# Edge tiles over 64 nodes with fixed node ranges in a four-layer graph network kernel

## The chip, the core and the metric

The kernel runs on one core of a Trainium2 chip, as one program and one launch. The metric is device microseconds per execution. TensorE multiplies matrices, VectorE and ScalarE do elementwise work and reductions, GpSimd does some elementwise work and issues the indirect gathers, and SyncE issues most of the other transfers.

## The reference

Four layers over a graph of N = 2048 nodes, for B = 8 batches of D = 64 features. The adjacency `adj` is an integer matrix, symmetric, with ones on its diagonal; it is random and sparse (each of the two halves that are joined has a chance of 0.00195 per entry, so a node has about nine neighbours). After each layer the input is added and a layer norm follows.

```python
# layer 0, attention with one score per side
h = layernorm((x * node_weights + node_bias + x) @ W) * gamma + beta
e = leaky_relu(s1[:, :, None] + s2[:, None, :], 0.2)     # s1 = h @ a1, s2 = h @ a2
out = elu(softmax(where(adj > 0, e, -9e15)) @ h + h)
# layer 1, softmax over the neighbours, for each feature by itself
feat = softplus(x * (w0 / sqrt(2)) + b0);  scores = feat * wa + ba
out = sum over j of softmax_j(where(adj, scores[j], -1e9)) * feat[j]
# layer 2, mean over the neighbours
out = layernorm(relu(x @ W_self + b_self + (adj @ x / deg) @ W_neigh + b_neigh))
# layer 3, four heads and a last layer, both with scores h_i . h_j over the neighbours
h = x @ Wh[head].T;  out_h = softmax(where(adj, h @ h.T, -1e16)) @ h      # for 4 heads
h2 = leaky_relu(concat(out_h), 0.2) @ Wo.T
out2 = softmax(where(adj, h2 @ h2.T, -1e16)) @ h2 + bo
out = layernorm(leaky_relu(out2, 0.2)) * gamma + beta
# after each layer: x = layernorm(x + out)
```

## The kernel before

The nodes form 16 node tiles of 128 (`P`). All neighbours of a node tile are put into **edge tiles** of 128 slots, one slot for one edge. A node tile is cut into `NG` groups of `GN` = 32 nodes, and each group has `GS` = 3 edge tiles, 384 slots (`GE`). A group's two halves of `GH` = 16 nodes each start at a fixed slot, 0 and 192: so the first edge tile holds edges of the first half only, the second of either half, and the third of the second half only. `src` (L173) holds for each slot the row of the source node, `SelT` the matrix from nodes to slots, and `Sel` its transpose. `gather` (L186) is an indirect transfer that GpSimd issues: it fetches for the 128 slots of an edge tile the rows of their source nodes from a table in device memory. A node tile takes 12 gathers.

The program's stages, in order:

- **Adjacency and node products (L303 to L383).** For each node tile VectorE finds the neighbours in the adjacency rows (`key`, `MAX8`), TensorE counts the slots ahead of each node (`pl`, L354), VectorE makes `offs` and `ends`, `first_of` (L362) and `SelT` (L363), TensorE spreads the lists to the slots (`pl`, `ps`, L369 and L370), ScalarE copies `Sel` (L371), and VectorE reads each slot's neighbour out (`hit`, `at_`, `src`). A matrix form of the adjacency, `ET`, is kept for the first `DENSE` node tiles. The products of layer 0 run in between.
- **Layer 0 (L385 to L470).** For each node tile: 12 gathers into `hs` (two buffers), scores, weights, `weigh` (L421: VectorE multiplies the gathered rows by the weights, L428, and TensorE sums them with `self_`, a copy of `Sel`, into `po`, and the weights into `pd`), `divide`, residual and norm. While the gathers of a node tile go out, the one before is worked on.
- **Layer 1 and layer 2 sums (L556 to L620, L880 to L945).** The first `DENSE` = 9 node tiles are summed by dense matmuls with `ET` (L556, L915; 24 and 12 of 512 columns in a batch). The other node tiles are summed by list: gathers of `rs`, then matmuls with `self_` (L608, L895) in "quads" of four edge tiles, one of each group, that write four different column groups of 32. TensorE's order alternates dense batches with quads.
- **Heads of layer 3 (L954 to L1190).** For each edge tile: `fetch` the rows `xs`, `turn` them (four transposes into `pt`, L1000, and a copy `xsT` on ScalarE, L1002), `score` (matmuls `pscore`, L1015, an exp on ScalarE, L1018, and a mask by `Sel` on VectorE, L1024), and `back` (matmuls of the weights with the rows into `po`, L1041, and a copy into `o` on VectorE, L1046). Edge tiles 0 and 2 of a group, each over 16 nodes, form one step, and edge tile 1, over 32 nodes, the next; there are eight steps per node tile. Beside them runs the work of whole node tiles: `turn_nodes` (transposes of X), `sides` (`quarters` L970 and copies into `U`), `through_w` (`quarters` of `o`, and z), `sums` (a transpose of the softmax sums, L1058, and reciprocals), `through_wo` (L1076, and h2 on VectorE and GpSimd) and `pieces` (three bfloat16 parts of h2). The order on TensorE, ScalarE, VectorE and GpSimd is the order of the program, written out by hand: `turn(k+2)`, work aside, `score(k+1)`, `back(k)`. `beside` says which work stands in which step j of a node tile. The PSUM banks: `pt` one, `pscore` two buffers of two banks, `po` one, `pm` (for `quarters`, Wo and `turn_nodes`) two.
- **Last layer (L1186 to L1345).** Units of two gathers, six per node tile: TensorE expands the nodes' own rows to the slots (`pe`, L1210), VectorE multiplies (`pr`, L1215) and reduces (`sc`, L1220), ScalarE takes the exp, the weighting `wx` is shared by VectorE and ScalarE in two units of three and done by GpSimd in the third (L1231, L1236), and TensorE adds up (`po`, `pd`, L1248, L1250). The end work of a node tile (`divide`, `leaky`, `take_stats`, `normalise`, ...) stands at fixed units after it. Here too the order is the program's.

At the end a few operations see whether any node had too many neighbours, or any slot range ran over; in that case a slower program for any input runs (`nbad`, L1354 and after).

Of the kernel before, what the change touches and what calls it, by code (L numbers as in the profile page):

```python
# [32 lines left out]
P = 128  # L33
# [15 lines left out]
def kernel(ctx: ExitStack, tc: tile.TileContext, ins: dict, out: bass.AP):  # L49
# [12 lines left out]
    GN = 32  # L62
    GH = 16
    NG = P // GN
    GS = 3
    GE = GS * P
    SL = 24

# [99 lines left out]
    room = main.tile([P, 1], F32, name="room")  # L168
# [3 lines left out]
    Sel = main.tile([P, NT, GS, P], FP8, name="Sel")  # L172
    src = main.tile([P, NT, GS, NG], U32, name="src")  # L173
    recs = main.tile([P, NT, HN + 1, B], F32, name="recs")
# [7 lines left out]
    DENSE = 9  # L182
# [122 lines left out]
    nc.vector.tensor_scalar(before, before, 0.0, None, op0=ALU.is_gt)  # L305
    half_i = aw.tile([P, 1], I32, name="half_i")
    nc.gpsimd.iota(half_i, pattern=[[0, 1]], base=0, channel_multiplier=1)
    nc.vector.tensor_scalar(half_i, half_i, 4, None, op0=ALU.logical_shift_right)
    half_no = aw.tile([P, 1], F32, name="half_no")
    nc.vector.tensor_copy(half_no, half_i)  # L310
    halves = aw.tile([P, P // GH, GH], F32, name="halves")
    nc.gpsimd.iota(halves, pattern=[[1, P // GH], [0, GH]], base=0, channel_multiplier=0, allow_small_or_imprecise_dtypes=True)
    nc.vector.scalar_tensor_tensor(before, halves.rearrange("p a b -> p (a b)"), half_no, before,
                                   op0=ALU.is_equal, op1=ALU.mult)
    nc.vector.tensor_scalar(half_i, half_i, 1, None, op0=ALU.bitwise_and)
    half0 = aw.tile([P, 1], F32, name="half0")
    nc.vector.tensor_copy(half0, half_i)
    nc.vector.tensor_scalar(half0, half0, GE / 2, None, op0=ALU.mult)
    nc.vector.tensor_scalar(room, half0, GE / 2, None, op0=ALU.add)
# [3 lines left out]
    for it in range(NT):  # L323
# [28 lines left out]
        pl = aps.tile([P, 1 + GS * NG * (SL + 1)], F32, name="pl", bufs=1)  # L352
        poff = pl[:, 0:1]
        nc.tensor.matmul(poff, before, deg[:, it:it + 1], start=True, stop=True)  # L354
        nc.vector.tensor_scalar(offs[:, it:it + 1], poff, half0, 2.0 * GE, op0=ALU.add, op1=ALU.min)
# [9 lines left out]
        pl = pl[:, 1:].rearrange("p (g l) -> p g l", l=SL + 1)  # L365
        ps = aps.tile([P, GS, P], F32, name="ps", bufs=1)
# [4 lines left out]
        nc.scalar.activation(Sel[:, it], ps, AF.Copy, saturate=False)  # L371
# [7 lines left out]
        nc.vector.tensor_reduce(at_.rearrange("p s g -> p (s g)"), hit, AX.X, ALU.add)  # L379
        nc.vector.tensor_scalar(src[:, it], at_, -1.0, 0.0, op0=ALU.add, op1=ALU.max)  # L380
# [13 lines left out]
    def fetch(it):  # L394
# [6 lines left out]
        self_ = wk.tile([P, GS, P], F32, name="self_")  # L401
# [19 lines left out]
    def weigh(it):  # L421
        hs, self_, w, wm = held[it]
        po = ps_o.tile([P, BD], F32, name="po")
        pd = ps_w.tile([P, NG, B], F32, name="pd")
        for s in range(GS):
            own = slice(s * NG, (s + 1) * NG)
            wx = hs[:, own].rearrange("p g b d -> p (g b) d")
            nc.vector.tensor_tensor(wx, wx, along(w[:, own].rearrange("p g b -> p (g b)")), ALU.mult)  # L428
            nc.tensor.matmul(pd, self_[:, s], wm[:, own], start=(s == 0), stop=(s == GS - 1))
            for g in range(NG):  # L430
                nodes = slice(g * GN, (g + 1) * GN)
                nc.tensor.matmul(po[nodes], self_[:, s, nodes], hs[:, s * NG + g].rearrange("p b d -> p (b d)"),
                                 start=(s == 0), stop=(s == GS - 1))
        held[it] = po, pd

    def divide(it):
        po, pd = held.pop(it)
        den = wk.tile([P, NG, B], F32, name="den")
        nc.vector.tensor_tensor(den, pd, group.unsqueeze(2).to_broadcast(den.shape), ALU.mult)
        rd = wk.tile([P, B], F32, name="rd")  # L440
        nc.vector.tensor_reduce(rd, den.rearrange("p g b -> p b g"), AX.X, ALU.add)
        nc.vector.reciprocal(rd, rd)
        z = zs[it] = po.rearrange("p (b d) -> p b d", d=D)
        for b in range(B):
            nc.scalar.activation(z[:, b], z[:, b], AF.Copy, scale=rd[:, b:b + 1])
# [55 lines left out]
    with ExitStack() as l1:  # L501
# [87 lines left out]
        quads = [(it, s) for it in range(NT - 1, DENSE - 1, -1) for s in range(GS)]  # L589
        rss, selfs = {}, {}  # L590

        def fetch(n):
            if n < len(quads):
                it, s = quads[n]
                rss[n] = [gk.tile([P, 2, BD], F32, name="rs") for _ in range(NG)]
                for g in range(NG):
                    gather(rss[n][g].rearrange("p h n -> p (h n)"), rtab, it, s, g)

        def add_edges(n):
            it, s = quads[n]  # L600
            if s == 0:
                selfs[it] = wk.tile([P, GS, P], F32, name="self_")
                nc.scalar.activation(selfs[it], Sel[:, it], AF.Copy)
                sums[it] = new_sums()
            for h in range(2):
                for g in range(NG):
                    nodes = slice(g * GN, (g + 1) * GN)
                    nc.tensor.matmul(sums[it][h][nodes].rearrange("p a f -> p (a f)"), selfs[it][:, s, nodes],  # L608
                                     rss[n][g][:, h], start=(s == 0), stop=(s == GS - 1))
            if s == GS - 1:  # L610
# [26 lines left out]
    f3w = fast.enter_context(tc.tile_pool(name="f3w", bufs=1))  # L637
    early = ExitStack()
# [13 lines left out]

    def turn_nodes(it):
# [4 lines left out]
        nc.scalar.copy(xTs[it], px.rearrange("p a n -> p (a n)"))  # L658
        for k in range(2):
            nc.vector.memset(xTs[it][k * D:k * D + 1], 1.0)  # L660
# [51 lines left out]
    with ExitStack() as l2:  # L712
# [160 lines left out]
        quads = [(it, s) for it in by_list for s in range(GS)]  # L873

        def selection(n):
            if n < len(by_list):
                it = by_list[n]
                selfs[it] = wk.tile([P, GS, P], F32, name="self_", bufs=3)
                nc.scalar.activation(selfs[it], Sel[:, it], AF.Copy)

        def fetch(n):
            if n < len(quads):
                it, s = quads[n]
                rss[n] = [gk.tile([P, BD], F32, name="rs") for _ in range(NG)]
                for g in range(NG):
                    gather(rss[n][g], ytab, it, s, g)

        def add_edges(n):
            it, s = quads[n]
            if s == 0:  # L890
                selection(by_list.index(it) + 2)
                sums[it] = pa.tile([P, BD], F32, name="pa")
            for g in range(NG):
                nodes = slice(g * GN, (g + 1) * GN)
                nc.tensor.matmul(sums[it][nodes], selfs[it][:, s, nodes], rss[n][g], start=(s == 0), stop=(s == GS - 1))  # L895
            if s == GS - 1:
# [55 lines left out]
    with early, ExitStack() as heads:  # L952
        wk = heads.enter_context(tc.tile_pool(name="f3s", bufs=2))
        gk = heads.enter_context(tc.tile_pool(name="f3g", bufs=13))  # L954
        ps_t = heads.enter_context(tc.tile_pool(name="f3pst", bufs=1, space=PSUM))
        ps_s = heads.enter_context(tc.tile_pool(name="f3pss", bufs=2, space=PSUM))
        ps_o = heads.enter_context(tc.tile_pool(name="f3pso", bufs=1, space=PSUM))
# [3 lines left out]
        def quarters(W, v, hs, pool=None):  # L961


            pq = pool.tile([P, 2, 2, 2, P], F32, name="pscore") if pool else ps_m.tile([P, 2, 2, 2, P], F32, name="pm")
# [17 lines left out]


        NODES = [(0, GH), (0, GN), (GH, GH)]
        PARTS = ((0, 2), (1,))
        steps = [(it, g, ss) for it in range(NT) for g in range(NG) for ss in PARTS]

        def fetch(k):
            it, g, ss = steps[k]
            xss[k] = [gk.tile([P, BD], F32, name="xs") for _ in ss]  # L990
# [927 lines left out]
```

## Time and profile before

| | |
|---|---|
| median of 3 runs | 2062.78 us (2061.77 to 2065.36) |
| span of the profiled execution | 2152.0 us |
| TensorE busy | 1601.9 us, 74% |
| VectorE busy | 1410.2 us, 66% |
| GpSimd busy | 1065.8 us, 50% |
| ScalarE busy | 1024.4 us, 48% |
| moved by DMA | 283.66 MB, 132 GB/s in the mean |

The profile is one execution taken by the hardware profiler; its span is 4.3% above the median of the runs. The page gives no other time for the profiled execution than this span, so every sum over profile rows is to be compared with 2152.0. Its busy shares are averages over stages with different limits, so the stages have to be read one by one: in the profile, the adjacency stage runs from 0 to 205 us, layer 0 to 511, layer 1's rows to 615, layer 1's sums to 786, layer 2's node products to 841, layer 2's sums to 1037, the heads to 1728, the last layer to the end. Rows of groups give line, engine, operation, out<-in, shapes and count, then busy time and mean nanoseconds of one, then the idle time ahead and what ended it. Float32 matmuls show as two records each, and durations of TensorE records overlap, so the text takes the distance of their starts.

### The profile page before, as it was taken

How to read it: one execution, taken by the hardware profiler on the slowest of the kernel's cores; microseconds unless marked ns; L12 is line 12 of the kernel's file. 1: busy time of each engine (PE TensorE's matmuls, PEld its weight loads, DVE VectorE, ACT ScalarE, POOL GpSimd, SP SyncE). 2: the span in 40 equal slices, each digit the busy share in tenths (PEclk: the TensorE clock that was granted, in tenths of full speed). 3: DMA queues.
4: the chain of work that ended last, by engine and by line, in shares of the span. 5: the costliest groups of instructions: out<-in, count | busy, mean ns of one | idle time of the engine just before them, and what ended most of it. 6: DMA issues, size and time to landing. Idle time of an engine off the chain costs nothing. (4 is left out here: it accounts for less than half of the span.)

```text
span 2152.0 us, 35076 instructions
## 1 busy us (share of the span) xinstructions
PE 1601.9 (74%) x13062; PEld 921.8 (43%) x13062; DVE 1410.2 (66%) x3027; ACT 1024.4 (48%) x2506; POOL 1065.8 (50%) x997
## 2 busy tenths in 40 slices
PE   3562334442799988876599999899999859888873
PEld 3552111110333345222487777777777712222220
DVE  6887477876664466467255555555555569898986
ACT  4542134346822243364354444444444436677774
POOL 0001766661655536554445455545544367777760
PEclk9755666555999999998599999999999955555555
DMA  7422666550258833554333223323322155555541
GB/s 197 142 85 73 198 181 183 176 176 23 96 181 292 303 114 110 161 150 118 90 90 113 78 89 99 103 83 98 99 84 84 60 168 166 162 168 170 164 120 27
DMA packets 134243, 283.66 MB, mean 132 GB/s; under 512 B 64144, under 2 KB 66704, under 8 KB 131984
## 3 DMA queue, kind: packets, MB, share of 16 engines
q0 software_dynamic: 64896, 217.10, 33.4%
q1 hardware_dynamic: 52528, 60.03, 8.3%
q10 hardware_dynamic: 16640, 4.20, 0.9%
q8 instruction: 105, 1.72, 0.3%
q14 instruction: 74, 0.61, 0.1%
HBM read 245.35 MB, written 35.91 MB: 131 GB/s over the span
## 5 line engine op out<-in xcount | busy, mean ns | idle before, releaser
L186 POOL DMA_INDIRECT hs<-htab,src x192 | 183.8, 957 | 290.6 <-PE pe L408 202.8
L1024 DVE SCALAR_TENSOR_TENSOR w<-w,Sel 128x512 f32<-128x512 f32 (+1 forms) x192 | 188.6, 1009 | 193.8 <-ACT w L1018 192.8
L186 POOL DMA_INDIRECT xs<-xtab,src x192 | 216.4, 1127 | 76.3 <-issue 39.0
L556 PE MATMUL pa<-R,ET 128*128 128x512 bf16 x864 | 198.9, 388 | 51.9 <-POOL R L544 35.0
L1015 PE MATMUL pscore<-U,xsT 64*128 64x64 f32 (+1 forms) x3072 | 224.2, 288 | 10.4 <-issue 7.9
L186 POOL DMA_INDIRECT hs<-ktab,src x192 | 188.7, 983 | 53.8 <-issue 46.6
L1015 PEld LDWEIGHTS pscore<-U,xsT 64*128 64x128 f32 x3072 | 198.4, 196 | 36.4 <-issue 25.7
L1018 ACT ACTIVATE w<-pscore 128x1024 f32<-128x1024 f32 x128 | 131.0, 1023 | 144.7 <-PE pscore L1015 112.1
L1002 ACT COPY xsT<-pt 128x512 f32<-128x512 f32 x192 | 112.1, 584 | 178.5 <-PE pt L1000 134.6
L1041 PE MATMUL po<-w,xs 128*64 128x64 f32 (+1 forms) x3072 | 159.6, 251 | 17.6 <-DVE o L1046 13.4
L151 ACT ACTIVATE X<-X,ln_m,ln_r 128x64 f32<-128x64 f32 x256 | 87.2, 428 | 171.3 <-DVE ln_m L143 66.9
L1086 POOL TENSOR_TENSOR h<-h,h2h 128x512 f32<-128x512 f32 x45 | 57.1, 1269 | 221.3 <-DVE h2h L1082 221.0
L1210 PE MATMUL pe<-hi,selTb 32*128 32x512 bf16 x576 | 135.9, 606 | 35.0 <-DVE pr L1215 26.2
L556 PEld LDWEIGHTS <-ET 128*128 128x128 fp8e4 x864 | 84.1, 99 | 174.3 <-issue 82.5
L1041 PEld LDWEIGHTS po<-w,xs 128*64 128x64 f32 x3072 | 127.5, 142 | 52.4 <-issue 28.9
L1000 PE MATMUL pt<-ident,xs 128*128 128x128 f32 x768 | 134.3, 301 | 20.5 <-DMA xs<-xtab,src 12.3
L1215 DVE TENSOR_TENSOR pr<-pe,hs 128x1024 f32<-128x1024 f32 x96 | 116.9, 1218 | 18.2 <-DMA hs<-ktab,src 9.9
L1231 ACT ACTIVATE wx<-hs,w 128x64 f32<-128x64 f32 x512 | 128.7, 341 | 0.0
L1220 DVE TENSOR_REDUCE sc<-pr 128x16 f32<-128x1024 f32 x96 | 116.6, 1215 | 4.3 <-ACT w L1222 1.2
L186 POOL DMA_INDIRECT rs<-rtab,src x84 | 79.7, 949 | 72.2 <-PE pa L608 52.1
L1000 PEld LDWEIGHTS pt<-ident,xs 128*128 128x128 f32 x768 | 86.1, 148 | 49.0 <-issue 13.3
L428 DVE TENSOR_TENSOR hs<-hs,w 128x2048 f32<-128x2048 f32 x48 | 106.8, 2279 | 0.5 <-ACT w L418 0.5
(597 smaller groups left out, 3243.1 us busy)
## 6 DMA issues: line engine op xcount, KB each, us to landing
at<-in_adj SPq DMA_DIRECT2D x16, 1024.0 KB
rtab<-r SPq DMA_DIRECT2D x16, 512.0 KB
ptab<-hp SPq DMA_DIRECT2D x16, 384.0 KB
hi<-ptab SPq DMA_DIRECT2D x16, 384.0 KB
X<-in_x ACTq DMA_DIRECT2D x16, 256.0 KB
htab<-H SPq DMA_DIRECT2D x16, 256.0 KB
ytab<-y SPq DMA_DIRECT2D x16, 256.0 KB
ktab<-hb SPq DMA_DIRECT2D x16, 256.0 KB
```

Source lines behind the costliest of these rows:

```text
L186: nc.gpsimd.indirect_dma_start(out=dst, out_offset=None, in_=table[:, :], in_offset=bass.IndirectOffsetOnAxis(ap=src[:, it, s, g:g + 1], a ...
L556: nc.tensor.matmul(po[h].rearrange("p a f -> p (a f)"), ET[:, jt, it * P:(it + 1) * P], R[:, jt, q, h].rearrange("p a f -> p (a f)"), star ...
L1000: nc.tensor.transpose(pt[:, p], xss[k][n][:, p * P:(p + 1) * P], ident)
L1002: nc.scalar.copy(xsT, pt)
L1015: nc.tensor.matmul(pscore[:, k_, f0:f0 + HN * ni].rearrange("p (h i) -> p h i", i=ni), xsTs[k][t][half, p], Us[it][half, p, :, i0:i0 + ni] ...
L1018: nc.scalar.activation(w.rearrange("p t k a h i -> p k t (a h i)"), pscore.rearrange("p k (t m) -> p k t m", t=n), AF.Exp)
L1024: nc.vector.scalar_tensor_tensor(wt, wt, 3.0e38, edge, op0=ALU.min, op1=ALU.mult)
L1041: nc.tensor.matmul(po[half, p, :, i0:i0 + ni], xss[k][t][:, f0:f0 + D], ws[k][:, t, k_, p], start=(s == 0 and p == 0), stop=(last and p == ...
L1210: nc.tensor.matmul(pe[:, k].rearrange("p b d -> p (b d)"), selTb[nodes, s * P:(s + 1) * P], hi[nodes, q], start=(q == 0), stop=(q == 2))
L1215: nc.vector.tensor_tensor(pr.rearrange("p k b d -> p (k b d)"), pes[u].rearrange("p k b d -> p (k b d)"), hss[u].rearrange("p k b d -> p ( ...
L1220: nc.vector.tensor_reduce(sc, pr, AX.X, ALU.add)
L1231: nc.scalar.activation(wxs[u][:, 0, b], hss[u][:, 0, b], AF.Copy, scale=ws[u][:, 0, b:b + 1])
```

## The change

Groups get 64 nodes (`GN`), so there are two per node tile, with five edge tiles each (`GS`, 640 slots): ten gathers per node tile instead of twelve. Each edge tile may hold edges of a fixed range of nodes only (`WINDOWS`: 0 to 20, 10 to 32, 20 to 44, 32 to 54, 44 to 64 of the 64). The lower 32 nodes (a "block") fill the slots from the front, the upper 32 from the end. A selection matrix is kept per pair of edge tile and block, `QS`, six per group: edge tile 2 belongs to both blocks. All sums write 32 output rows at a time; `TOGETHER` puts edge tiles 0 and 3, 1 and 4, and 2 together, so that a round again writes four column groups.

In layer 0, `pd` is summed per block, so that `den` and its reduction are left out. Layers 1 and 2 take 8 node tiles by matrix (`DENSE`) and 8 by list. In the heads a step is one edge tile, in the order 0, 2, 1, 4, 3, ten steps per node tile; `back` stands one step later (after `score(k+1)` comes `back(k-1)`); the sums of a block have a `po` bank each of two; `quarters` moves from `pm` to the buffers of `pscore`, `sums` from `ps_t` to `pm`, which now has one bank; one piece of work aside stands in each step; the ones in `xT` come from ScalarE's copy (scale and bias) instead of two memsets on VectorE; z is copied by ScalarE, and VectorE takes the maximum of z and 0.2 z. In the last layer a unit is the two gathers of one edge tile number, five units per node tile. The checks at the end also count each group's edges and the offsets from the end.

```diff
-    GN = 32
-    GH = 16
+    GN = 64
+    GB = 32
     NG = P // GN
-    GS = 3
+    GS = 5
...
+    WINDOWS = [(0, 20), (10, 32), (20, 44), (32, 54), (44, 64)]
+    def blocks_of(s):
+        a, b = WINDOWS[s]
+        return [(k, max(a, k * GB), min(b, (k + 1) * GB)) for k in range(GN // GB) if a < (k + 1) * GB and b > k * GB]
...
+    TOGETHER = ((0, 3), (1, 4), (2,))
+    QS = [(s, x[0]) for s in range(GS) for x in blocks_of(s)]
...
-    Sel = main.tile([P, NT, GS, P], FP8, name="Sel")
+    Sel = main.tile([P, NT, NG, NQ, GB], FP8, name="Sel")
...
-    DENSE = 9
+    DENSE = 8
...
-        nc.vector.tensor_scalar(offs[:, it:it + 1], poff, half0, 2.0 * GE, op0=ALU.add, op1=ALU.min)
+        nc.vector.tensor_scalar(offs[:, it:it + 1], poff, -1.5 * GE, 2.0 * GE, op0=ALU.max, op1=ALU.min)
+        nc.vector.tensor_tensor(offs[:, it:it + 1], offs[:, it:it + 1], base, ALU.add)
...
-        nc.scalar.activation(Sel[:, it], ps, AF.Copy, saturate=False)
+        for k in range(GN // GB):
+            of = [q for q, x in enumerate(QS) if x[1] == k]
+            nc.scalar.activation(Sel[:, it, :, of[0]:of[-1] + 1].rearrange("p g q n -> p q g n"),
...
+        nc.vector.tensor_scalar(at_, at_, float(N), None, op0=ALU.min)
...
     def weigh(it):
...
-        pd = ps_w.tile([P, NG, B], F32, name="pd")
-        for s in range(GS):
-            own = slice(s * NG, (s + 1) * NG)
...
+        pd = ps_w.tile([P, B], F32, name="pd")
+        for n, ss in enumerate(TOGETHER):
+            for s in ss:
+                own = slice(s * NG, (s + 1) * NG)
+                wx = hs[:, own].rearrange("p g b d -> p (g b) d")
+                nc.vector.tensor_tensor(wx, wx, along(w[:, own].rearrange("p g b -> p (g b)")), ALU.mult)
...
     def divide(it):
-        den = wk.tile([P, NG, B], F32, name="den")
-        nc.vector.tensor_tensor(den, pd, group.unsqueeze(2).to_broadcast(den.shape), ALU.mult)
-        nc.vector.tensor_reduce(rd, den.rearrange("p g b -> p b g"), AX.X, ALU.add)
-        nc.vector.reciprocal(rd, rd)
+        nc.vector.reciprocal(rd, pd)
...
-        nc.scalar.copy(xTs[it], px.rearrange("p a n -> p (a n)"))
-        for k in range(2):
-            nc.vector.memset(xTs[it][k * D:k * D + 1], 1.0)
+        nc.scalar.activation(xTs[it], px.rearrange("p a n -> p (a n)"), AF.Identity, scale=keep[:, 0:1], bias=keep[:, 1:2])
...
-        quads = [(it, s) for it in by_list for s in range(GS)]
+        quads = [(it, c) for it in by_list for c in range(len(TOGETHER))]
...
-        gk = heads.enter_context(tc.tile_pool(name="f3g", bufs=13))
+        gk = heads.enter_context(tc.tile_pool(name="f3g", bufs=12))
-        ps_o = heads.enter_context(tc.tile_pool(name="f3pso", bufs=1, space=PSUM))
+        ps_o = heads.enter_context(tc.tile_pool(name="f3pso", bufs=2, space=PSUM))
...
-            pq = pool.tile([P, 2, 2, 2, P], F32, name="pscore") if pool else ps_m.tile([P, 2, 2, 2, P], F32, name="pm")
+            pq = ps_s.tile([P, 2, 2, 2, P], F32, name="pscore")
...
-        NODES = [(0, GH), (0, GN), (GH, GH)]
-        PARTS = ((0, 2), (1,))
-        steps = [(it, g, ss) for it in range(NT) for g in range(NG) for ss in PARTS]
+        TURN = (0, 2, 1, 4, 3)
+        steps = [(it, g, s) for it in range(NT) for g in range(NG) for s in TURN]
+        OPEN, CLOSE = (0, 2), (1, 3)
...
-            pd = ps_t.tile([P, 2 * HN * NP], F32, name="pt")
+            pd = pool.tile([P, 2 * HN * NP], F32, name="pt") if pool else misc([P, 2 * HN * NP])
...
-            nc.scalar.activation(z.rearrange(flat), pn.rearrange(flat), AF.Relu, scale=0.8)
-            nc.vector.scalar_tensor_tensor(z.rearrange(flat), pn.rearrange(flat), 0.2, z.rearrange(flat), op0=ALU.mult, op1=ALU.add)
+            nc.scalar.copy(z.rearrange(flat), pn.rearrange(flat))
+            nc.vector.scalar_tensor_tensor(z.rearrange(flat), z.rearrange(flat), 0.2, z.rearrange(flat), op0=ALU.mult, op1=ALU.max)
...
-            0: lambda it: ([(turn_nodes, it + 1)], []),
-            1: lambda it: ([(through_w, it - 1, 0)], []),
-            2: lambda it: ([(sums, it - 1)], [(through_wo, it - 1, 0)]),
-            3: lambda it: ([(through_wo, it - 1, 1)], [(through_w, it - 1, 2)]),
-            4: lambda it: ([], [(through_wo, it - 1, 2)]),
-            5: lambda it: ([(through_wo, it - 1, 3)], [(sides, it + 1, 0)]),
-            6: lambda it: ([], [(sides, it + 1, 2)]),
-            7: lambda it: ([(pieces, it - 1)], []),
+            0: (turn_nodes, 1), 1: (through_w, -1, 0), 2: (sides, 1, 0), 3: (through_w, -1, 2), 4: (through_wo, -1, 0),
+            5: (through_wo, -1, 1), 6: (sides, 1, 2), 7: (through_wo, -1, 2), 8: (through_wo, -1, 3), 9: (pieces, -1),
...
-        AHEAD = 6
+        AHEAD = 7
...
-            for k in range(len(steps)):
+            for k in range(len(steps) + 1):
...
-                    turn(k + 2, 0)
-                it = steps[k][0]
-                aside(k % (NG * len(PARTS)), it, 0)
+                    turn(k + 2)
+                it, j = divmod(k, PER)
+                if j == 4 and 0 < it < NT:
+                    sums(it - 1)
+                f, t, *a = beside[j]
+                if k < len(steps) and 0 <= it + t < NT:
+                    f(it + t, *a)
                 if k + 1 < len(steps):
                     score(k + 1)
-                if k + 2 < len(steps):
-                    turn(k + 2, 1)
-                aside(k % (NG * len(PARTS)), it, 1)
-                back(k)
+                if k:
+                    back(k - 1)
...
-        units = [(it, s, g) for it in range(NT) for s in range(GS) for g in range(0, NG, 2)]
+        units = [(it, s) for it in range(NT) for s in range(GS)]
...
-        PER = GS * NG // 2
+        PER = GS
...
-        lack = fp.tile([P, 3, NT], F32, name="lack")
+        lack = fp.tile([P, 5, NT], F32, name="lack")
```

## The prediction

> **What bounds the kernel now.** I read the chain that ended last first: no engine has over 9% of it and no line over 4%, so there is no single bound and the work goes stage by stage. The table of busy time by stretch comes next. Its columns are the stretch, its length, the busy time of TensorE, weight loads, VectorE, ScalarE and GpSimd, then the granted clock, the DMA share and GB/s.
>
> ```profile
> 0.00:205.00 205.00, 95.00 (x594) 83.98 (x594) 170.36 (x696) 92.81 (x157) 3.24 (x12) 0.72 0.40 124
> 205.00:511.00 306.00, 126.55 (x576) 49.57 (x576) 215.68 (x389) 103.82 (x322) 183.80 (x192) 0.59 0.56 165
> 615.00:786.00 171.00, 166.74 (x917) 63.75 (x914) 94.64 (x239) 41.10 (x119) 79.51 (x95) 1.00 0.76 259
> 841.00:1037.00 196.00, 146.19 (x660) 52.28 (x658) 114.95 (x417) 88.73 (x242) 97.01 (x105) 0.88 0.46 133
> 1037.00:1728.00 691.00, 630.32 (x8506) 520.29 (x8507) 359.48 (x486) 312.52 (x433) 335.12 (x283) 0.93 0.30 91
> 1728.00:2152.00 424.00, 325.00 (x1334) 88.71 (x1333) 353.42 (x665) 276.44 (x1070) 278.54 (x247) 0.52 0.50 144
> ```
>
> These are A (adjacency and node products; VectorE), B (layer 0), D (layer 1 sums; TensorE 97%), F (layer 2 sums; TensorE and gathers), G (heads of layer 3; TensorE 91%) and H (its last layer; VectorE 83%). The two stretches between them have no edge tiles. In A, VectorE idles only 14 us at the start and otherwise for short waits.
>
> In B no engine is full. GpSimd's waits there:
>
> ```profile
> POOL hs L186 <- issue: 51.5, 169, 0.3
> POOL hs L186 <- remote: 33.9, 14, 3.1
> ```
>
> Gathers leave back to back, 0.96 us busy and 0.30 of issue each, and stop once per node tile for 2.4 us before its first one. `hs` has two buffers, so that stop is the older node tile's sums giving its buffer back. A node tile takes 17.3 us.
>
> In G, a timeline of TensorE shows what an edge tile costs (start, busy time, group; I use start to start):
>
> ```profile
> 1446.69 1.09 PE L1041 MATMUL po<-w,xs 128*64 128x128 f32 x16
> 1447.72 0.66 PE L1000 MATMUL pt<-ident,xs 128*128 128x128 f32 x4
> 1448.31 1.16 PE L1015 MATMUL pscore<-U,xsT 64*128 64x128 f32 x16
> ...
> 1451.06 1.15 PE L1041 MATMUL po<-w,xs 128*64 128x64 f32 x32
> 1452.14 0.66 PE L1000 MATMUL pt<-ident,xs 128*128 128x128 f32 x4
> 1452.63 1.06 PE L1076 MATMUL pm<-WoT,z 128*128 128x128 f32 x8
> 1453.62 2.00 PE L1015 MATMUL pscore<-U,xsT 64*128 64x64 f32 x32
> ```
>
> A 32-node tile (x16) scores in 1.14 us and sums in 1.03. Two 16-node tiles (x32) score in 1.93 and sum in 1.08: 0.97 and 0.54 each. And what TensorE waits for over the 16 node tiles:
>
> ```profile
> PE po L1041 <- DVE o L1046: 13.4, 15, 1.4
> PE pt L1058 <- ACT xsT L1002: 11.1, 15, 0.9
> PE pscore L1015 <- issue: 7.5, 29, 0.5
> PE po L1041 <- issue: 3.8, 15, 0.3
> ```
>
> In H, a unit of two gathers costs VectorE a product, a reduction and, in two units of three, a weighting; VectorE is busy for 21 to 22 of each node tile's 24 us.
>
> ```profile
> L1215 DVE TENSOR_TENSOR pr<-pe,hs 128x1024 f32<-128x1024 f32 x94 | 114.4, 1217 | 8.3 <-issue 5.2 <-PE pe L1210 3.1
> L1220 DVE TENSOR_REDUCE sc<-pr 128x16 f32<-128x1024 f32 x94 | 114.2, 1215 | 4.3 <-ACT w L1222 1.2
> L1236 DVE TENSOR_TENSOR wx<-hs,w_ps 128x512 f32<-128x512 f32 x62 | 41.4, 668 | 0.0
> ```
>
> **What the Trainium skill says.** "TensorE: Matmul & The Clock Gate", Part 1: the granted clock is full or half, decided over free-running windows of about 3.41 us, and an idle window halves it. The trace agrees: in G the clock record steps between 1.0 and 0.5 in multiples of 3.41 us, with eight drops. The same page, "LDWEIGHTS": a load costs by its columns. Score loads always have 128, and going from 64 to 128 moving columns raises a tile from 0.97 to only 1.14 us, so I read 0.97 as the loads' floor. The same page, Part 3: small tiles in different column groups run together. In D, 16 records of 599 ns, over four groups of 32 columns, take 1.93 us; the trace agrees.
>
> **The change part by part**, in microseconds of the profiled execution (span 2152.0). The median of the runs, 2062.78, is 0.9585 of that.
>
> *A: +5.* Rows of 640 slots instead of 384. `first_of` (0.30 for 384) and `SelT` (0.61) grow by 0.09 and 0.27 if only about 0.15 of each is fixed; the shorter `hit` (240 elements, was 288; two of 0.44) gives back 0.15; the added offset operation and the `min` are 0.06 each at the price of this stage's smallest rows. That is +0.33 by 16. Two more `pl`/`ps` pairs on TensorE and a split selection copy on ScalarE lie in waits for VectorE. Bounds +2 to +9.
>
> *B: -27.* Ten gathers instead of twelve: 2 x 1.26 = 2.5 us less of GpSimd per node tile. The buffer's loop for two node tiles is now gathers 15.1, landing 3, weights 3.9, first product 2.2, matmuls 10.3: 34.5. TensorE's order still has three rounds over four column groups, products split from 3 x 2.28 into 5 x about 1.2, `den` and its reduction (0.4 on VectorE) are gone: about 31 for two, 15.6 each. GpSimd alone would need 12.6 + 2.2 = 14.8, VectorE 13.5 - 1.2 = 12.3. 17.3 - 15.6 = 1.7, by 16. Bounds -40 (VectorE's limit nearly reached) to -18.
>
> *D: -13.* A node tile by matrix less is 6 x 16 = 96 matmuls of 512 columns at 0.2224 start to start: -21.4. One more node tile by list is 3 rounds x 1.93: +5.8. A node tile's ten gathers of 0.5 MB in a list period of 16.8 us (was 21.4 with twelve) ask 312 GB/s where 290 to 305 now flow at a DMA share of 0.85 to 0.90. I take 2.5 us for that. Bounds -15.5 and -3.
>
> *F: -6.* 48 matmuls at 0.2216 = -10.6, three rounds of 1.0 = +3.0. TensorE already waits 17.9 us here for gathers, and what is shorter may be waited for: bounds -16 and +4, and I take 1.6 off the gain.
>
> *G: -46.* A node tile's work on TensorE now: turns 12 x 0.52 = 6.2, scores 4 x (1.13 + 1.93) = 12.2, sums 4 x (1.03 + 1.08) = 8.4, `quarters` 4.1, Wo 4.0, rest 0.7: 35.6. Waits for `o` 0.84 and `xsT` 0.69, issue 0.7 give 37.9. It measures 41.0, and the clock's 0.93 accounts for the other 3.1. After: turns 5.2; ten scores 80 to 96 columns wide, 1.02 each between the two prices above: 10.2; sums 0.66 at 80 and 0.72 at 88 columns, and the tile across both blocks twice 0.54: 3.84 per group, 7.7; the rest 8.8: 31.9. The wait for `o` goes with the second bank, that for `xsT` with `sums` leaving `ps_t`. Two new ones come. At j=1 `through_w` needs the last copy of `o`. `back` now runs a step later, and on VectorE that copy (0.68) stands behind the next score's mask, which waits for its exp; one `turn` covers 0.5 of it: about 1.6. At j=4 `sums` and the Wo product share the one bank of `pm`: Wo waits for three reciprocals (0.25, 0.15, 0.15), queued behind z (1.2) and a mask: about 1.7. On ScalarE, `pieces` one step after the last Wo waits for GpSimd's h (1.27) and holds back an exp by about 1.5; the score buffer hides most. VectorE (some 20 us per node tile) and GpSimd (10 x 1.13 + 3 x 1.27) stay below. 31.9 + 3.3 + issue 0.7 + clock 2.2 = 38.1, 2.9 less by 16. The clock is the guess: bounds 36 and 41, that is -80 and 0.
>
> *H: -46.* Sixteen units fewer, each 1.22 + 1.22 + 0.67 x 2/3 = 2.86 on VectorE, less 0.09 overlap that start to start shows at most. Per node tile the others stay below its 21: GpSimd 17.5 falls, ScalarE 17.6, TensorE 18. If VectorE's waits for `leaky` grow, -38; with one saved, -55.
>
> End: four small operations, +0.5. Two gathers fewer per node tile in G cost nothing and save nothing: GpSimd has 335 of 691 there. The moved SP transfers of `o` leave a step later, but have two steps more until `sums`.
>
> Sum: 5 - 27 - 13 - 6 - 46 - 46 + 0.5 = -132.5. Taken off the median as it is, 1930; scaled by 0.9585, 1936. I say **1932**.
>
> **Rivals.** *The heads gain nothing.* Two stalls of about 1.6 us, each next to transposes, fall into 3.41-us windows and halve the clock once more per node tile, 3 us: 41 again. For it: eight drops came already with issue gaps of 0.2 to 0.3 us in a row. Against it: TensorE still has 80% or more in each step. -86.5: about 1977.
> *Slower.* The same gate stays shut: at a mean clock of 0.75 in G a node tile is 31.9/0.75 + 4 = 46.5, and all other gains are gone (5.5 x 16 = 88); at 0.72 it is 48.3, and the kernel takes about 2090. For it: B and H run at 0.59 and 0.52 already. Against it: G's work has no idle window.
> *Layer 0 is bound elsewhere*, by landing or by TensorE at half clock: B gains nothing, 1958.
> *It doesn't do what it says*: were a group too full for its 640 slots, the fallback would run, and the time would be several times as long. The fullest group of these inputs has 616 edges.
>
> **How the numbers follow.** The forecast and layer 0's rival are 0.77 together, the heads' 0.16, slower 0.06, the fallback 0.01. The range takes G at 36.5 to 41 and the bounds of B and F half-way: 1885 to 1985. About 0.2% (4 us) is what a measurement here can tell from no change. Faster 0.92, same 0.01, slower 0.07.
>
> **What would show it.** Right: G near 38 us per node tile with new waits of TensorE for `o` at `quarters` and for the reciprocals before Wo, none at L1041; B near 280 us with the stop of GpSimd remaining; H near 378 with VectorE's rows x80; D near 158. Wrong: a granted clock below 0.85 in G, a B that stays at 306, or waits for `rs` in D.

## The result, and the profile after

The changed kernel takes **1989.23 us** in the median of four runs (1984.70 to 1994.99), where the kernel before takes 2063.16 on the same chip: a ratio of 0.9638, 95% interval 0.9616 to 0.9660. It is 74 us faster, not 131, and lies 4 us above the range of the prediction.

The profiled execution of after took 1989.1 us from first to last instruction, as long as its runs, whereas the profile of before (2152.0) was 89 us longer than the runs shown with it. The table of busy time by stretch of after (stretch, its length, busy time of TensorE, weight loads, VectorE, ScalarE and GpSimd, clock, DMA share, GB/s), for layer 0, the sums of layers 1 and 2, the heads and the last layer:

```profile
209.00:455.00 246.00, 119.85 (x928) 70.92 (x929) 194.07 (x389) 107.29 (x326) 153.14 (x160) 0.70 0.60 173
557.00:714.00 157.00, 153.53 (x876) 56.61 (x874) 95.05 (x234) 36.71 (x104) 76.73 (x91) 1.00 0.75 269
773.00:951.00 178.00, 134.98 (x638) 47.48 (x636) 112.35 (x415) 89.98 (x244) 93.59 (x102) 0.87 0.50 142
951.00:1598.00 647.00, 576.15 (x7854) 476.02 (x7855) 331.21 (x416) 286.91 (x431) 304.74 (x250) 0.91 0.28 83
1598.00:1989.00 391.00, 210.85 (x1252) 63.70 (x1251) 330.65 (x634) 255.48 (x957) 240.14 (x210) 0.75 0.47 136
```

Against the profile of before each of these stretches is shorter, the heads too (647 us, 691 before). That comparison misleads, as the experiments show. What TensorE waits for in the heads of after:

```profile
PE pscore L1014 <- DVE o L1080: 37.5, 15, 3.0
PE pm L1110 <- DVE recs L1097: 24.1, 15, 1.6
```

The two old waits (for `o` at the sums, for `xsT`) are gone. The two that were foreseen, at step 1 and at step 4 of a node tile, are there, 2.5 and 1.6 us each. The timeline of TensorE around the first of them (start, busy time, group):

```profile
1305.98 0.83 PE L1073 MATMUL po<-w,xs 128*64 128x88 f32 x16
1306.73 0.66 PE L1038 MATMUL pt<-ident,xs 128*128 128x128 f32 x4
1309.91 1.09 PE L1014 MATMUL pscore<-o,AT 64*64 64x256 f32 x16 [2.52 <-DVE o L1080]
1310.94 1.92 PE L1051 MATMUL pscore<-U,xsT 64*128 64x88 f32 x16
1312.79 1.33 PE L1073 MATMUL po<-w,xs 128*64 128x80 f32 x16
1314.05 1.12 PE L1038 MATMUL pt<-ident,xs 128*128 128x128 f32 x4
```

After the wait of 2.52 us a score takes 1.92 us instead of 1.13, a sum 1.33 instead of 0.78, a turn 1.12 instead of 0.66: TensorE runs at half clock. The clock record has 0.5 there for 6.8 us from 1311.1 on, two of its steps of 3.41 us. So a wait shorter than one such step can be enough.

### The profile page after: what moved, and what is told of

It reads as the page before. It is cut to its first block, busy times and chain, and to the rows that moved or that the text cites. A ratio compares the mean times of both kernels' runs of the same rounds, so it can differ in the third digit from the quotient of the medians.

```text
span 1989.1 us, 33903 instructions
## 1 busy us (share of the span) xinstructions
PE 1402.3 (70%) x12656; PEld 866.1 (44%) x12656; DVE 1338.7 (67%) x2975; ACT 981.0 (49%) x2405; POOL 958.6 (48%) x889
## 4 chain that ended last, share of the span: by engine, by line
PE 36%; DVE 15%; ACT 11%; issue 6%; POOL 3%; DMA 1%; ACTq 0%; SPq 0%; POOLq 0%; DVEq 0%
PE pscore L1051 8%; PE po L1073 5%; PE pa L588 5%; PE pt L1038 4%; PE pscore L1014 4%; PE pm L1110 3%; ACT z L169 2%; PE pa L643 2%; PE py L789 2%; ACT wx L1256 2%; DVE w L1057 2%; DVE sc L1245 1%; DVE st L155 1%; POOL hs L203 1%; PE pa L959 1%
## 5 line engine op out<-in xcount | busy, mean ns | idle before, releaser
L203 POOL DMA_INDIRECT hs<-htab,src x160 | 153.1, 957 | 265.6 <-ACT selTf L431 207.0
L1057 DVE SCALAR_TENSOR_TENSOR w<-w,Sel 128x640 f32<-128x640 f32 (+2 forms) x160 | 169.2, 1064 | 147.5 <-ACT w L1054 147.4
L203 POOL DMA_INDIRECT xs<-xtab,src x160 | 184.6, 1154 | 55.3 <-issue 32.0
L1051 PE MATMUL pscore<-U,xsT 64*128 64x80 f32 (+2 forms) x2560 | 198.3, 299 | 0.0
L1054 ACT ACTIVATE w<-pscore 128x640 f32<-128x640 f32 (+2 forms) x160 | 119.7, 748 | 150.9 <-PE pscore L1051 150.0
L203 POOL DMA_INDIRECT hs<-ktab,src x160 | 159.6, 998 | 45.5 <-issue 37.4
L1073 PE MATMUL po<-w,xs 128*64 128x88 f32 (+2 forms) x3072 | 147.7, 245 | 0.7 <-DVE w L1057 0.7
L1235 PE MATMUL pe<-hi,selTb 64*128 64x512 bf16 x480 | 87.0, 480 | 75.7 <-DVE pr L1240 67.3
L1240 DVE TENSOR_TENSOR pr<-pe,hs 128x1024 f32<-128x1024 f32 x80 | 97.4, 1217 | 14.4 <-DMA hs<-ktab,src 9.9
L597 DVE RECIPROCAL rec<-pa 128x256 f32<-128x256 f32 x32 | 54.2, 1731 | 64.2 <-PE pa L643 38.0
L460 DVE TENSOR_TENSOR hs<-hs,w 128x1024 f32<-128x1024 f32 x80 | 91.9, 1215 | 3.1 <-ACT w L449 3.1
```

The lines of the kernel that those rows point to most:

```text
L203: nc.gpsimd.indirect_dma_start(out=dst, out_offset=None, in_=table[:, :], in_offset=bass.IndirectOffsetOnAxis(ap=src[:, it, s, g:g + 1], a ...
L1051: nc.tensor.matmul(pscore[:, k_, f0:f0 + HN * ni].rearrange("p (h i) -> p h i", i=ni), xsT[half, p], Us[it][half, p, :, i0:i0 + ni], start ...
L1054: nc.scalar.activation(w.rearrange("p k a h i -> p k (a h i)"), pscore[:, :, 0:NP * HN * ni], AF.Exp)
L1057: nc.vector.scalar_tensor_tensor(wt, wt, 3.0e38, edge, op0=ALU.min, op1=ALU.mult)
L1073: nc.tensor.matmul(po[half, p, :, a - blk * GB:b - blk * GB], xs[:, f0:f0 + D], w[:, k_, p, :, a - WINDOWS[s][0]:b - WINDOWS[s][0]], start ...
L1240: nc.vector.tensor_tensor(pr.rearrange("p k b d -> p (k b d)"), pes[u].rearrange("p k b d -> p (k b d)"), hss[u].rearrange("p k b d -> p ( ...
```

## The experiments

Each experiment ran on one chip, side by side with the kernel before. Three levels were met, by the median of before: 2063 to 2065 us (the result, and e9 to e11), 2155 (e12), and 2189 to 2191 (e1 to e8, called the slow chip). Which chip the result ran on is not known; e9 to e11 are set beside it because they are at its level.

**Before, profiled again** (e1, e5, e9; no edit).

> The kernel before, unchanged, profiled a second time. Theory 1 (the 89 us by which the first profile of before lay above its runs is a loss of that one execution, at half clock in layer 0 and the last layer): the new span is near 2062, layer 0 takes about 265 us instead of 306, the last layer about 395 instead of 427, the heads 665 as before; then layer 0 and the last layer gained some 20 and 5 us by the change, not 61 and 36. Rival (profiling makes this kernel slower each time): again about 2150 with the same stages, and the missing gain is elsewhere. Third: the excess lies in the heads, which then take about 580 to 600 and were not made faster at all.

It took 2192.49 where the median of before beside it was 2190.98: 130 us above the runs that the prediction was scaled to, with the heads at 695 us (664.5 in the first profile, cut alike). The first two theories fall: the excess is no accident of one execution, and not the profiler's, since timed runs on this chip are as long. The third, the heads, is left to a profile on a quicker chip. The first profile's 2152.0 lies where the runs of before at the level of 2155 do (2150 to 2160); on which chip it was taken is not known.

> The kernel before, unchanged, on whatever chip this lands on. If it is one where the kernel before takes about 2063: the first profile there. Theory (TensorE's supply of instructions is worse on the chip of the profile): no row of issue gaps in layer 0, which then takes about 270, the heads about 640, the other stages as before. If it takes about 2190: the same stages as the second profile of before, within 15 us each.

> The kernel before, unchanged, once more, in search of a chip where it takes about 2063. There, theory (TensorE's rows of issue gaps, 20 us in layer 0, 24 in the heads and 12 in the last layer on the chip seen so far, are absent, and with them part of the half-clock windows): layer 0 about 275, layer 2 sums about 208, the heads about 640, the last layer about 415. On the chip seen so far: 2190 again.

e5 met the slow chip (2191.35) and repeats e1 within 2 us in every stage. e9 met the level of the result (2059.24 beside a median of 2065.15). There layer 0 took 295 us (275 expected), layer 2's sums 208 (208), the heads 607 (640), the last layer 427 (415): the third theory of e1 was nearest, though layer 0 fell by 26 us too (321.5 in the first profile, cut alike). Heads of before, by stretch, first on the slow chip (e1), then at the level of the result (e9):

```profile
1068.00:1763.00 695.00, 635.48 (x8423) 527.06 (x8423) 355.64 (x477) 307.56 (x425) 310.29 (x269) 0.92 0.28 85
```

```profile
1023.00:1630.00 607.00, 574.73 (x8424) 480.58 (x8423) 353.06 (x473) 306.96 (x425) 327.38 (x270) 0.99 0.33 98
```

The same instructions take 88 us less, at a clock of 0.99 instead of 0.92. TensorE's waits there, e1 and then e9:

```profile
PE pscore L1015 <- issue: 16.9, 56, 1.0
PE pt L1058 <- ACT xsT L1002: 11.0, 15, 0.7
PE po L1041 <- DVE o L1046: 8.7, 14, 1.0
PE po L1041 <- issue: 7.2, 15, 1.0
```

```profile
PE po L1041 <- DVE o L1046: 15.1, 14, 1.5
PE pt L1058 <- ACT xsT L1002: 11.0, 15, 0.7
```

The waits by program remain: over the whole stage 10.1 us in e1 and 16.5 in e9 for `o`, 11.0 in both for `xsT`. What goes is "issue", gaps for which the trace shows no cause (24 us), and with it the half-clock time, 114 us of the stretch in e1 and 7 in e9. If half of that time is lost, gaps and clock make some 78 of the 88 us. I had read those gaps in the profile of before as part of the kernel. The stages of both kernels at both levels, cut at the first instruction of each (start, first gather of layer 0, first dense product of layer 1, first gather of layer 1, first dense product of layer 2, first `po` sum of the heads, first `pe`, end):

| us | predicted | before e9 | after | change | before e1 | after e6 | change |
|---|---|---|---|---|---|---|---|
| adjacency | +5 | 206.1 | 211.0 | +4.9 | 205.1 | 211.0 | +5.9 |
| layer 0 | -27 | 295.3 | 260.6 | -34.7 | 325.8 | 285.7 | -40.1 |
| layer 1 rows | 0 | 84.8 | 84.9 | +0.1 | 84.8 | 84.8 | 0 |
| layer 1 sums, layer 2 products | -13 | 229.0 | 216.3 | -12.7 | 230.6 | 217.0 | -13.6 |
| layer 2 sums, lead into the heads | -6 | 207.9 | 192.1 | -15.8 | 221.7 | 205.2 | -16.5 |
| heads | -46 | 607.3 | 633.2 | **+25.9** | 695.0 | 645.6 | -49.4 |
| last layer, end | -45.5 | 427.0 | 390.9 | -36.1 | 427.6 | 389.8 | -37.8 |
| sum | -132.5 | 2057.4 | 1989.1 | -68.3 | 2190.6 | 2039.1 | -151.5 |

**After, on the slow chip** (e6; no edit).

> The changed kernel, unchanged, beside a run of the kernel before on the same chip. Theory (the ratio hangs on the chip: where before takes 2190, it loses time in layer 0 and the heads that the changed kernel loses only in part): about 2030 where before takes 2190, a ratio of 0.925 to 0.93; 0.964 again where it takes 2063. Rival (the ratio is the same on every chip): 0.964 on both.

2042.50 beside 2189.28, ratio 0.9324 (0.9299 to 0.9348): a little above the theory's 0.925 to 0.93, and far from the rival's 0.964. The change is worth twice as much on that chip. Its heads show no row of issue gaps there, where before has 24 us: each node tile has two real waits instead. Why these two waits come without issue gaps is not shown. In layer 0 the gaps are there in both kernels (23 us in e1, 40 in e6).

**through_w a step later** (e2, slow chip).

```diff
-            0: (turn_nodes, 1), 1: (through_w, -1, 0), 2: (sides, 1, 0), 3: ...
+            0: (turn_nodes, 1), 1: (sides, 1, 0), 2: (through_w, -1, 0), 3: ...
```

> The changed kernel, with through_w(0) at step 2 and sides(0) at step 1 of a node tile. TensorE's wait for the last copy of o (37.5 us in all, 2.5 each) goes, and with it a half-clock window per node tile. Theory (the new stall and the clock drop it draws cost the heads what they cost in the profile): 37 us of waits and some 15 of clock, 45 to 55 us faster, about 1940. Rival (the wait only moves: TensorE then waits for xT before sides, or for z at step 3, or for the sums of softmax later): at most 10 us faster.

2045.77, no faster than e6's 2042.50 on the same chip, where the theory had 45 to 55 us. The wait for `o` is gone, and that for the reciprocals fell from 24.0 to 16.7 us, but 28 us of issue gaps have come, at one place in nearly every node tile, the two-block sum of step 2, and half-clock time after them. The timeline there:

```profile
1326.27 0.67 PE L1073 MATMUL po<-w,xs 128*64 128x48 f32 x9
1327.36 0.39 PE L1073 MATMUL po<-w,xs 128*64 128x48 f32 x6 [0.42 <-issue]
1328.12 0.35 PE L1073 MATMUL po<-w,xs 128*64 128x48 f32 x5 [0.37 <-issue]
1328.89 0.33 PE L1073 MATMUL po<-w,xs 128*64 128x48 f32 x4 [0.42 <-issue]
```

**sums a step sooner** (e3 on the slow chip, e11 at the level of the result).

```diff
-                if j == 4 and 0 < it < NT:
-                    sums(it - 1)
                 f, t, *a = beside[j]
                 if k < len(steps) and 0 <= it + t < NT:
                     f(it + t, *a)
+                if j == 3 and 0 < it < NT:
+                    sums(it - 1)
```

> The changed kernel, with sums at the end of step 3's work aside instead of the start of step 4, so that the three reciprocals have a score and a back to hide under before Wo needs the bank. Theory: the wait of TensorE for the reciprocals (24.1 us, 1.6 each) and part of a half-clock window go: 25 to 35 us faster, about 1958. Rival (the row sums have not come back from device memory by then, and TensorE waits for them instead): no gain, and a wait for dT in the trace.

> The kernel with the sums a step sooner once more, beside both moves. On the chip where before takes 2063: about 1950, 40 below the changed kernel, if its gain there is what it was on the other chip (47), about 1965 if only the waits themselves go (24).

1995.53 on the slow chip, 47 below e6, more than the 25 to 35 that were expected; 1952.13 at the other level, 37 below after (ratio to before 0.9462, 0.9444 to 0.9480), about as expected then. The wait for the reciprocals fell from 24.1 us to this (e11):

```profile
PE pm L1110 <- DVE recs L1097: 3.0, 15, 0.2
```

So 21 us of waits bring about twice that. In the heads of e11, cut as in the table, the half-clock time is 55 us, where after has 102: half of the difference is 24, and 21 + 24 is near the 42 us by which the heads got shorter (633.2 to 591.1).

**Both moves** (e4 on the slow chip, e10 at the level of the result).

> The changed kernel with both moves. Theory: the gains add up, 65 to 90 us, about 1910, the heads at 34 to 35 us per node tile and the granted clock there at 0.96 or more. Rival (TensorE is not what the heads wait for once the stalls go, but the gathers or VectorE): less than the better of the two alone plus 10 us.

> The kernel of both moves once more. On the chip where the kernel before takes 2063, theory (no issue gaps there, so that what the later through_w saves is not given back): heads near 580 and about 1930. Rival (the gaps follow the moves on any chip): about 15 us slower than sums_sooner alone on the same chip, as seen.

On the slow chip 2005.63, 10 above e3, where the theory had about 1910: the issue gaps are back (27 us). At the level of the result **1894.33**, ratio 0.9182 (0.9165 to 0.9199), 95 us below after, and 36 below the 1930 that was expected. The stretch of the heads in after and in e10, and the waits of e10 there:

```profile
965.00:1598.00 633.00, 566.89 (x7788) 468.27 (x7787) 329.68 (x415) 282.37 (x424) 294.22 (x240) 0.92 0.27 81
966.00:1499.00 533.00, 521.10 (x7772) 433.49 (x7769) 325.04 (x416) 281.38 (x423) 300.69 (x239) 0.99 0.33 96
```

```profile
PE pm L1092 <- DMA dT<-dtab: 4.8, 5, 1.7
PE pscore L1014 <- DVE o L1080: 1.4, 1, 1.4
PE pm L1110 <- DVE recs L1097: 1.4, 7, 0.2
```

TensorE has the same work as in after (x7772, x7788 there) and takes 100 us less. From e11 to e10 the wait for `o` went from 38.9 to 1.4 us, about 35 us of waits in all, and the half-clock time from 55 to 7: 35 + 24 is near the 58 us by which the heads got shorter. Both moves beat the change at both levels: the ratio is 0.9144 (0.9169 at most) on the slow chip, where after has 0.9324. There e3 alone is better still (0.9100).

**The wait kept, its idling filled** (e12, the level of 2155).

```diff
...
+                if j == 1 and 0 < it < NT:
+                    fill = misc([P, P])
+                    for _ in range(8):
+                        nc.tensor.matmul(fill, ident, ident, start=True, stop=True)
                 f, t, *a = beside[j]
...
```

The sums stand a step sooner here, as in e11.

> The kernel with the sums a step sooner, and eight needless 128x128 products (2 us at full clock, into a bank that is free then and never read) in TensorE's program between turn and through_w of step 1: the wait for the last o stays, but TensorE has something to multiply meanwhile. Theory (the wait costs as much again by the half-clock window that idling draws): the half-clock time in the heads falls from 64 us to about 20 and the heads are 15 to 25 us faster than sums_sooner alone, about 570 where that took 591, or 580 where it took 601. Rival (the half-clock windows come from the length of the step or from the transposes, not from idling): the clock stays and the heads take 591 or 601, or up to 10 more.

1974.75 beside 2155.12. The clock did what the theory said: 17 us of half-clock time in the heads, in the stage's first 17 and last 6 us, and none in the steady node tiles. (By the table's cut e11 has 55, not the 64 of the expectation.) The time did so only in part: 589.5 us, where the theory had 570 to 580 and e11 and e3 took 591 and 601. A steady node tile takes 36.5 us. In e11 it takes 35.7 if the clock holds and 37.2 to 39.2 if it drops, 37.7 in the mean over both. So the idle wait does draw the drop, and the drops cost 2.0 us per node tile in the mean; but the filled kernel loses 0.8 of that again. The rest of the gain goes outside the steady node tiles, where the filled kernel takes some 10 us more than e11. A timeline of TensorE in it:

```profile
1319.10 0.66 PE L1038 MATMUL pt<-ident,xs 128*128 128x128 f32 x4
1319.59 1.95 PE L1184 MATMUL pm<-ident 128*128 128x128 f32 x16
1322.28 1.09 PE L1014 MATMUL pscore<-o,AT 64*64 64x256 f32 x16 [0.74 <-DVE o L1080]
1323.31 1.13 PE L1051 MATMUL pscore<-U,xsT 64*128 64x88 f32 x16
...
1325.65 1.57 PE L1014 MATMUL pscore<-xT,G 64*64 64x256 f32 x16
1327.15 1.26 PE L1051 MATMUL pscore<-U,xsT 64*128 64x80 f32 x16
1328.35 1.27 PE L1073 MATMUL po<-w,xs 128*64 128x48 f32 x32
```

`quarters` still starts 3.2 us after the turn, as in e11, and the score behind it takes 1.13 us, not 1.92. But in step 2 `quarters` takes 1.57 instead of 1.09 and the sum 1.27 instead of 1.14, at a recorded clock of 1.00: this is where e2 had its issue gaps. The level of 2155 was met in this experiment alone, so the 0.8 and the 10 us may be that chip's.

**Nine node tiles by matrix** (e7, slow chip).

```diff
-    DENSE = 8
+    DENSE = 9
```

> The changed kernel with nine node tiles by matrix in layers 1 and 2, as before. Theory (each of the two layers was worth what the prediction's sum said): layer 1 sums 13 us slower, layer 2 sums 6 slower, the adjacency 2 slower, about 20 in all against the changed kernel on the same chip. Rival (what the matrix costs, the list now costs in gathers): within 5 us.

2063.56 beside e6's 2042.50, 21 slower by the medians, and the theory had 20; but its runs scatter from 2054 to 2079, and the profiled one is the fastest, 13 us longer than e6's. By stage: layer 1 sums +12.2 (the theory's 13), layer 2 sums +9.1 (not its 6), and adjacency -2.7, within the 208 to 213 us that this stage takes in runs which leave it alone; the heads, which the edit leaves alone too, were 8 us shorter. Against before on that chip (e5) it leaves layer 1 as it was (229.2, 229.4) and layer 2 shorter by 7.0 us. That fewer gathers bring those 7 is likely but not shown: TensorE's wait for `rs` there is no shorter (14.1 us in e5, 20.5 in e7).

**GpSimd's units by place** (e8, slow chip): units 0, 4 and 6 of ten.

```diff
-            if u % 3:
+            if u % 10 not in ON_POOL:      # ON_POOL = (0, 4, 6), at all five places
```

> The changed kernel, with the last layer's units whose weighting GpSimd does picked by their place in ten units (0, 4, 6) instead of every third. With six units per node tile the third always fell to the same place beside the norm's work on VectorE; with five it moves along, and in the trace ln_v takes up to 2.5 us while GpSimd weighs, 0.9 in the mean instead of 0.175. Theory (VectorE stands still while GpSimd reads two operands): ln_v back to about 0.2, leaky to about 1.0, the last layer 12 to 18 us faster. Rival (VectorE only waits there instead of elsewhere, or the seventh unit in ten on VectorE takes it back): within 4 us.

The rival held: the last layer takes 388.5 us, 389.8 in e6. (The median, 2033.75, is 9 us below e6's, but most of that lies in stages that the edit leaves alone.) `ln_v` fell from 1.03 to 0.41 us, but VectorE's idle time ahead of `wx` rose from 5.4 to 17.8, of which 10.3 has no cause in the trace.

## Why the prediction was wrong

**Scaling the profile: this step failed first.** I worked out the sum against 2152 and took it off 2063, whole or times 0.9585, as if the 89 us between them lay evenly. They lay in layer 0 (26 us), layer 2's sums (12) and the heads (57), by the first profile against e9. In the heads 11 us of issue gaps and half of 66 us of half clock, which e9 doesn't have, make 44 of the 57. So a part of what I counted as saved was not in the runs.

**Heads, the clock term: mis-sized from both sides.** Before, I put 3.1 us per node tile on the clock and 0.7 on issue gaps. At the level of the result the stretch is 607.3/16 = 38.0, at a clock of 0.99 with 7 us of half clock in all: 0.2 per node tile, and no issue gaps. Work and waits (35.6 + 0.84 + 0.69 = 37.1) are nearly all of it.

After, I put the clock at 2.2; 102 us of half clock, half of it lost, are 3.2. The work of 31.9 was near: e10, nearly without waits, takes a steady 33.1.

The waits came where they were foreseen, that for the reciprocals in its size (1.6, foreseen 1.7), that for `o` too short (2.5, foreseen 1.6). In the timeline above the two masks ahead of the copy of `o` took 3.52 us together, from 1305.74, instead of some 2, while GpSimd did the two operations of `pieces` (1.17 and 1.27 from 1305.31). So it is in 13 of the 16 node tiles: a mask beside both operations takes 2.65 us, one with no GpSimd product beside it at most 0.96 (105 of the 160 masks).

Sum: 31.9 + 4.1 + 3.2 = 39.2, measured 39.6. That is 1.6 slower than before where I had 2.9 faster, and 4.5 x 16 = 72 us is more than the whole miss of 57. Of the 4.5, 2.9 are the clock of before (3.1 to 0.2), 1.0 the clock of after (2.2 to 3.2) and 0.8 the waits of after (3.3 to 4.1), 0.2 too many in all. The clock is what turned the gain into a loss: the one steady node tile of after with no half clock took 37.1 us, those with 6.8 us of it 40.2 to 40.3, where before takes a steady 38.05.

The rival "the heads gain nothing" (1977) named the mechanism and came nearest, but it too started from 41.0. Part of the miss was made up by luck: layers 0 and 2 gave some 17 us more than I had, for reasons that I had not given.

**The page on the clock gate** of the Trainium skill ("TensorE: Matmul & The Clock Gate", Part 1) gives an idle window of about 3.4 us as the cause; without a length, it also tells of a kernel in which frequent short idles made the clock swing. Here waits of 2.5 and 1.6 us, next to transposes, were enough: 19 drops in the heads of after, two in e10. Not each wait draws a drop: e11 has 14 waits for `o` of 2.5 us and over, and ten drops, each within 1.6 us of the end of one. What decides between them no run here shows. The measurement decides against 3.4 us as the least that it takes. My case against the slower rival, that the heads have no idle window, was no bar to half-clock windows.

**Layer 0** gained 35, not 27, and not for the reason that I gave. By gathers a node tile went from 15.35 to 13.3 us: 2.0, of the 2.5 of two gathers. At this level GpSimd's issue binds, and its stop for the older buffer is only 0.4 us per node tile before (e9) and 0.8 after:

```profile
POOL hs L186 <- PE po L432: 6.4, 11, 0.9
```

```profile
POOL hs L203 <- PE pd L468: 12.6, 8, 2.7
```

The loop through the two buffers that I summed to 34.5 is that of the first profile and of the slow chip (17.5 to 15.1 per node tile there).

**Layer 1** is right to 0.3 us, in part by luck. The sums got 14.4 us shorter (168.4 to 154.0). The 2.5 us that I took off for gathers don't show, since TensorE has no wait for `rs` there; 1.7 came back in layer 2's products, which I had at nothing. **Layer 2** gained 16 where I took 6. The sums gave 9.2 (155.7 to 146.5), where my prices without the 1.6 for waits make 7.6; the wait for gathers stayed as it was (e9, then after).

```profile
PE pa L895 <- DMA rs<-ytab,src: 15.3, 5, 6.8
```

```profile
PE pa L939 <- DMA rs<-ytab,src: 15.0, 5, 5.8
```

The other 6.6 lie between the last of these sums and the first `po` of the heads (52.2 to 45.6), a stretch that I had put at nothing.

**Last layer**: the 46 us are in VectorE's rows for the units (by my own prices, 2.86 less 0.09 and by 16, it would have been 44), and 10 came back elsewhere. The rows of VectorE, e9 and then after:

```profile
L1262 DVE SCALAR_TENSOR_TENSOR z<-z 128x512 f32<-128x512 f32 x15 | 15.2, 1016 | 27.7 <-ACT z L1259 27.7
L140 DVE SCALAR_TENSOR_TENSOR ln_v<-st,eps 128x16 f32<-128x16 f32 x14 | 2.4, 175 | 0.5
L123 DVE SCALAR_TENSOR_TENSOR ln_r<-ln_v,guess 128x16 int32<-128x16 int32 x14 | 2.4, 174 | 0.5
```

```profile
L1288 DVE SCALAR_TENSOR_TENSOR z<-z 128x512 f32<-128x512 f32 x15 | 18.8, 1251 | 14.7 <-ACT z L1285 14.6
L158 DVE SCALAR_TENSOR_TENSOR ln_v<-st,eps 128x16 f32<-128x16 f32 x14 | 12.7, 908 | 0.5
L141 DVE SCALAR_TENSOR_TENSOR ln_r<-ln_v,guess 128x16 int32<-128x16 int32 x14 | 7.3, 521 | 0.5
```

One `ln_v` of 2.50 us, from 1780.49, ends with GpSimd's weighting of 1.91 us from 1781.03. The "GPSIMD Engine Reference" of the Trainium skill, Specifications, says that GpSimd shares its SBUF interfaces with VectorE, with contention when VectorE reads two operands from SBUF. The trace agrees: in the last layer of after, the 12 of 18 `ln_v` with no GpSimd product beside them take 0.17 or 0.18 us, and the five beside one for over 1 us take 1.18 to 2.50. With five units per node tile every third unit no longer falls to a fixed place beside that work. But e8 shows that this is not what ends the stage: VectorE then waits elsewhere. What holds it some 10 us above the sum is open.

**Open** is what the issue gaps are. They are in layer 0, the heads and the last layer on one chip and all but absent on another, for the same program, and they follow the program's places (e2, e4). That instructions arrive late would fit; no run separates it.

## What to carry to other kernels

Before a profile is used as the base of a sum, hold its span against the runs: where the difference is not small beside the effect sought (89 us beside 131 here), the profile can hold losses that the runs don't have, and here they sat in single stages, not evenly. On a nearly full TensorE, price a new wait at 1.7 to 2 times its length, as it was here (35 us gave 58, 21 gave 42), and look for a step with slack for the work that waits: moving two calls by one step each was worth more than the whole change at the level of the result (95 us, 74). A move that empties TensorE's waits can be given back to issue gaps on another chip, so time it on more than one.

## What the runs showed of the hardware

- One program, unchanged, takes 2059 to 2067, 2150 to 2160 or 2187 to 2195 us at the three levels met, within 0.5% at each. Changed, it takes 1985 to 1995 or 2037 to 2046.
- Waits of 2.5 us, one per node tile, drew half-clock windows of 3.4 or 6.8 us in ten of 14 cases (e11); with eight 128x128 products in the wait, the clock stayed full in every steady node tile (e12).
- A VectorE operation of 0.17 us took up to 2.50 us beside one GpSimd product of 1.91 us, and a mask of some 0.9 us took 2.65 beside two of 1.17 and 1.27 (after).
